# Attention and feed-forward on one core: Q of groups 2 to 5 by pairs of heads, as 2x2 blocks in seven block products, with the sums on GpSimd

## The chip, the cores and the metric

The kernel runs on one core of a Trainium2 chip. The core has five engines with a queue of instructions each: TensorE (PE in the profile; PEld is its load of weights, which overlaps), VectorE (DVE), ScalarE (ACT), GpSimd (POOL) and SyncE (SP), which here only issues DMA transfers. An engine works through its queue in order and waits at an instruction until what it depends on is there. PSUM is the memory that TensorE writes into, in banks of 128 x 512 floats; SBUF is the working memory.

The metric is the time of one launch on the device in microseconds (us); the median of the runs counts.

## What is computed

Two layers on x of shape (2, 512, 512): attention with 32 query heads and 8 key/value heads of 128, causal softmax, an output projection, a residual and a layer norm; then a feed-forward of a base matrix and eight low-rank experts with a sparse routing, a residual and a layer norm. All in float32. Cut to what matters for the change:

```python
q = (x @ Wq).reshape(B, S, 32, 128).transpose(0, 2, 1, 3)     # B=2, S=512, HIDDEN=512
k = jnp.repeat((x @ Wk).reshape(B, S, 8, 128).transpose(0, 2, 1, 3), 4, axis=1)
v = jnp.repeat((x @ Wv).reshape(B, S, 8, 128).transpose(0, 2, 1, 3), 4, axis=1)
scores = jnp.where(causal, jnp.einsum('bhqd,bhkd->bhqk', q, k) * scale, -inf)
out = jnp.einsum('bhqk,bhkd->bhqd', jax.nn.softmax(scores), v)
x = layernorm(x + out.transpose(0, 2, 1, 3).reshape(B, S, 4096) @ Wo)
x = layernorm(x + ffn(x))
```

## The kernel before

Float32 accuracy comes from float16 matmuls: every operand is kept as a high and a low float16 part, and a product is three matmuls (high x high, high x low, low x high) that add up in one PSUM bank (`mm3`, L227). The weights are scaled by a power of two for each tile and then cut into the two parts by GpSimd (`split16`, L115: a scaling at L119, the high part at L121, the low part at L122). A result in PSUM is cut by ScalarE (high part, L234) and VectorE (low part, L235) in `cut_psum`.

The work goes over the 8 key/value heads ("groups" g, with 4 query heads each) and the two batches b: (0,0), (0,1), (1,0), ..., (5,1), then (6,0), (7,0), (6,1), (7,1). Each (g, b) has four units i = 0 to 3, one for each 128 query rows. One step of the main loop (L947) has, in the order in which the program is written:

- `unit_a` (L332) of this unit: the scores of four heads into banks `s`, the row maxima on VectorE (L395), the exponential on ScalarE (L400), and the cut of the weights of the softmax into the tile `phl` (ScalarE L359, VectorE L362), a transpose by DMA into `pt` after each half (`sync_transpose`, L388)
- one projection or two of the next (g, b): K and Q of head 0 in unit 0, Q of head 1 in unit 1, V in unit 2, Q of heads 2 and 3 in unit 3 (L956). Each is 12 matmuls of 512 columns (`project`, L242) into a bank of tag `pj`, of which there are two; the sums of squares `tot` (`total`, L127), from which the scales of the weights come, take banks of the same tag. After V, four copies and a transpose put its parts in order (`turn_v`, L301). `factors` (L256) puts five small GpSimd instructions (`lm`, L261 and L265) ahead of a group's products.
- `unit_b` (L415) of the unit before: softmax times V, `pv`
- `unit_c` (L456) of the unit before that: times Wo, `pw`, added into `acc` by VectorE (L469)

Between these stand the pieces of work that prepare weights for a later group: `prepare` (L159) loads six tiles (K, V, four of Q), `measure` (L176) takes their maxima on VectorE (L125), squares and sums them (`tot` on TensorE, `scales` on VectorE, L133), and `split16` cuts them. `at(generator, steps)` (used at L886 to L898) says in which steps of the main loop a piece is written into the program. The framework's scheduler then decides the order on each engine up to the tail, whose order is written out by hand (L910). The loads stand in SyncE's queue together with the transposes. The feed-forward's weights are loaded and prepared by `ffn_setup` (L474), on GpSimd above all, in the steps 20 to 36; its loads take buffers of the tag `raw`, which the projections' weights use too.

Of the kernel before, what the change touches and what calls it, by code (L numbers as in the profile page):

```python
# [25 lines left out]
NL = NE * NR + NE  # L26
SCALE = float(P) ** -0.5
# [4 lines left out]
TOP = 15  # L32
CUT = 2.0**-18
# [7 lines left out]
def kernel(  # L41
# [68 lines left out]
    def split(hi, lo, view):  # L110

        nc.gpsimd.tensor_scalar(hi, view, 1.0, 1.0, ALU.mult, ALU.mult)
        nc.gpsimd.tensor_tensor(lo, view, f(hi), ALU.subtract)
# [19 lines left out]
    def scales(sc, tot, n):  # L133

        nc.vector.tensor_scalar(
            tot[:, :n].bitcast(I32), tot[:, :n].bitcast(I32), 24, 23,
            ALU.logical_shift_right, ALU.logical_shift_left,
        )
        nc.vector.tensor_scalar(sc[:, 0, :n], tot[:, :n], 2.0**-109, 2.0 ** (64 - TOP), ALU.max, ALU.mult)
        nc.vector.reciprocal(sc[:, 1, :n], sc[:, 0, :n])  # L140
# [18 lines left out]
    def prepare(g, js, raws=None):  # L159

        if raws is None:
            raws = [load_raw(source(g, j), f"{g}_{j}", j >= 6) for j in js]
            yield
        name = f"{g}_{js[0]}"
        rows = js[0] >= 6
        n = 1 if rows else 6
        if (g, rows) not in SC:
            yield from measure(g, js, raws, name, rows, n)
        sc = SC[(g, rows)]
        for k, (j, raw) in enumerate(zip(js, raws)):  # L170
            j = 0 if rows else j
            LAST[(g, js[k])] = split16(*w_tile(g, js[k]), raw, sc[:, 1, j : j + 1], g == 0)
            if k % 2:
                yield

    def measure(g, js, raws, name, rows, n):  # L176
# [12 lines left out]
        scales(sc, total(sq, n, name), n)  # L189
        SC[(g, rows)] = sc  # L190
        yield

# [16 lines left out]
    def convert_x(b):  # L209

        raws = [load_raw(xt[b, :, c, :], f"x{b}_{c}") for c in range(KC)]
        yield
        yield from split_x(b, raws)

# [114 lines left out]

    PT = {}  # L330

    def unit_a(g, b, i, whole=True):  # L332
# [7 lines left out]
        phl = sb.tile([P, nb * P], F16, tag="PHL", name=f"phl{g}_{b}_{i}", bufs=2)  # L340
# [5 lines left out]
        def cut_p(h):  # L346
            nc.vector.reciprocal(st[:, 2, h : h + 2], st[:, 1, h : h + 2])
# [4 lines left out]
            for j in (h, h + 1):  # L352
                src, by = es[j], st[:, 3, j : j + 1]
                n = full + (j + 1) * R
                p = phl[:, (j * m + (j == 3)) * P :]
# [31 lines left out]
            on = slice(0, 2 * m) if h == 0 else slice(2 * m, nb)  # L387
            sync_transpose(pt[:, on], phl[:, on.start * P : on.stop * P])  # L388
# [85 lines left out]
    def ffn_setup():  # L474
# [6 lines left out]
        lars = [sb.tile([P, 512], F32, tag="raw", name=f"lraw{k}", bufs=6)[:, : half * NL] for k in range(2)]  # L481
        for k, lar in enumerate(lars):
            sync_load(lar.rearrange("p (c n) -> p c n", c=half), lar_in[:, k * half : (k + 1) * half, :])
        lraw = load_raw(lora_b, "lorab")
# [28 lines left out]
        scales(fsc, tot, 4)  # L513
# [360 lines left out]
    def first_rows():  # L874
        yield
        for k in (2, 3):
            w_squares(mx[:, 17 + k : 18 + k], wo_raw[k])
        amax(sq1[:, 1:2], mx[:, 17:21])
        tot = total(sq1[:, 1:2], 1, "2")
        sc = sb.tile([P, 2, 8], F32, tag="sc2", name="sc2")  # L880
        scales(sc, tot, 1)
        SC[(0, True)] = sc
        yield
        yield from prepare(0, ROWS, wo_raw)
# [5 lines left out]
    at(late_x(1, (1, 3)), 5, 6, 7, 7)  # L890
    at(ffn_setup(), 20, 21, 21, 21, 22, 22, 28, 28, 29, 29, 36)
    for g in range(1, NG):
        u = NT * (starts[g] - 2) - (3 if g == NG - 2 else 0)
        if g > 1:
            at(prepare(g, JS), u - (1 if g == NG - 2 else 2), u, u, u + 1, u + 2, u + 2, u + 3, u + 3, u + 3)
        u += NT
        if g > 1:
            at(prepare(g, ROWS), u - 2, u, u + 1, u + 2, u + 2, u + 3, u + 3)  # L898
# [48 lines left out]
    for s in range(len(units) - NT):  # L947
        if s < len(units):
# [6 lines left out]
            if nx:  # L955
                for j in ((4, 0), (1,), (5,), (2, 3))[i]:  # L956
                    proj(*nx, j)
# [72 lines left out]
```

## Time and profile before

| What | us |
|---|---|
| median of 3 runs (665.70 to 666.60) | 665.71 |
| the profiled execution, its own time | 665.56 |
| its span on the core (granted TensorE clock 0.999) | 663.7 |
| matmuls of `pw`, all 768 | 177.2 |
| matmuls of `pq`, all 672 | 152.4 |
| matmuls of `pv`, all 960 | 105.6 |
| matmuls of the scores, all 768 | 101.6 |
| GpSimd: low parts of weights (L122), 70 of 512 columns | 79.6 |
| GpSimd: scalings of weights (L119), 70 of 512 columns | 47.7 |
| GpSimd: high parts of weights (L121), 66 of 512 columns | 39.7 |

The durations of matmuls overlap one another (a matmul of 512 columns has 0.379 us, but its successor starts 0.216 us after it), so sums by group show shares, not time on a clock. Where time is meant, it is read from starts. The times of the four units of one group and batch in the middle of the program, busy time of each engine in each stretch:

```
stretch (us)    length  PE     DVE   ACT   POOL
282.90:293.70   10.80   10.80  5.60  4.32  2.44    unit 0
293.70:300.50    6.80    6.80  5.67  4.38  0.00    unit 1
300.50:308.70    8.20    8.20  7.17  6.56  1.42    unit 2
308.70:321.00   12.30   12.30  8.87  6.86  9.50    unit 3
```

A group takes the two batches, so about twice the sum of such a column. DMA issues of 256 KB land after 3.5 to 5.4 us by the page, the transposes after 3.7.

### The profile page before, as it was taken

What the parts mean: (1) busy time and instruction counts of PE and PEld (TensorE: products, weight loads), DVE (VectorE), ACT (ScalarE), POOL (GpSimd) and SP (SyncE); (2) the same over time, 40 slices, a digit from 0 to 9 for tenths busy, and PEclk for the clock granted to TensorE, in tenths of its full rate; (3) what the DMA queues carried; (4) which work ended last, traced back from release to release, by engine and by line L of the source; (5) the groups of instructions that cost most, each with busy time, mean ns of one, the idle gap of its engine ahead of it and who ended that gap; (6) DMA issues with size and microseconds to landing.
All of it is one profiled execution on the core that took longest, in us unless ns stands there. A gap on an engine that the chain in (4) does not pass through costs nothing.

```text
span 663.7 us, 12446 instructions
## 1 busy us (share of the span) xinstructions
PE 649.9 (98%) x3948; PEld 373.8 (56%) x3948; DVE 519.7 (78%) x1695; ACT 387.9 (58%) x1198; POOL 261.3 (39%) x411
## 2 busy tenths in 40 slices
PE   9999999999999999999999999999999999999995
PEld 5766556555555555555655555555555556555552
DVE  6797778868697787868698796868687687878796
ACT  6984755657375864747376474737566474545510
POOL 6885550806037199714127167054405001100011
PEclk9999999999999999999999999999999999999999
DMA  8859292827649393836739282754718263563321
GB/s 317 284 86 206 69 238 41 170 62 154 113 95 242 51 225 54 153 68 131 147 66 259 47 189 55 141 113 92 155 29 143 41 129 59 100 120 76 74 42 48
DMA packets 213538, 81.06 MB, mean 122 GB/s; under 512 B 198112, under 2 KB 198368, under 8 KB 213472
## 3 DMA queue, kind: packets, MB, share of 16 engines
q1 hardware_dynamic: 213472, 80.26, 57.4%
q8 instruction: 31, 0.51, 0.3%
q14 instruction: 35, 0.29, 0.1%
HBM read 29.12 MB, written 2.10 MB: 47 GB/s over the span
## 4 chain that ended last, share of the span: by engine, by line
PE 49%; DVE 9%; ACT 5%; issue 2%; DMA 1%; POOL 0%; POOLq 0%; ACTq 0%; DVEq 0%
PE pq L230 13%; PE pw L230 13%; PE pv L230 7%; PE s L230 7%; PE pk L230 4%; PE pvp L230 2%; ACT s L400 2%; DVE phl L362 2%; ACT phl L359 2%; PE pa L230 1%; DVE s L395 1%; DVE acc L469 1%; DMA pt<-phl 1%; DVE y L586 1%; DVE o L235 1%
## 5 line engine op out<-in xcount | busy, mean ns | idle before, releaser
L400 ACT ACTIVATE s<-s,ast 128x320 f32<-128x320 f32 (+15 forms) x256 | 117.8, 460 | 147.0 <-DVE ast L395 143.6
L230 PE MATMUL pw<-w,o 128*128 128x512 f16 x768 | 177.2, 379 | 0.3 <-DVE acc L469 0.3
L230 PEld LDWEIGHTS <-w 128*128 128x128 f16 x1008 | 98.0, 98 | 111.0 <-issue 0.2
L230 PE MATMUL pq<-xT,w 128*128 128x512 f16 x672 | 152.4, 379 | 0.0
L362 DVE SCALAR_TENSOR_TENSOR phl<-s,ast,phl 128x128 f16<-128x128 f32 (+7 forms) x352 | 125.2, 417 | 34.6 <-ACT phl L359 32.4
L359 ACT ACTIVATE phl<-s,ast 128x96 f16<-128x96 f32 (+11 forms) x304 | 117.6, 479 | 5.8 <-DVE ast L349 3.9
L230 PEld LDWEIGHTS <-o 128*128 128x128 f16 x768 | 74.9, 98 | 77.4 <-DVE o L235 0.7
L395 DVE CUSTOM_DVE_ANT_0 s<-s,mask,lm 128x320 f32<-128x320 f32 (+15 forms) x256 | 113.3, 502 | 0.4 <-PE s L230 0.4
L230 PE MATMUL pv<-pt,vt 128*128 128x256 f16 (+1 forms) x960 | 105.6, 262 | 1.0 <-DMA pt<-phl 1.0
L230 PE MATMUL s<-k,q 128*128 128x480 f16 (+15 forms) x768 | 101.6, 279 | 1.8 <-DVE phl L362 1.0
L230 PEld LDWEIGHTS <-vt 128*128 128x128 f16 x960 | 86.0, 99 | 20.7 <-issue 1.6
L230 PEld LDWEIGHTS <-q 128*128 128x128 f16 x768 | 62.5, 98 | 39.8 <-issue 2.7
L261 POOL TENSOR_SCALAR lm<-sc,xs 128x1 f32<-128x1 f32 x16 | 4.2, 265 | 193.9 <-DVE acc L469 101.7
L122 POOL TENSOR_TENSOR w<-raw,w 128x512 f16<-128x512 f32 x70 | 79.6, 1156 | 0.3
L119 POOL TENSOR_SCALAR raw<-raw,sc 128x512 f32<-128x512 f32 x70 | 47.7, 691 | 55.6 <-issue 40.9
L469 DVE SCALAR_TENSOR_TENSOR acc<-pw,lm,acc 128x512 f32<-128x512 f32 x64 | 47.7, 745 | 20.4 <-PE pw L230 20.2
L235 DVE SCALAR_TENSOR_TENSOR o<-pv,o 128x512 f16<-128x512 f32 x64 | 43.6, 681 | 24.3 <-ACT o L234 24.2
L234 ACT ACTIVATE o<-pv 128x512 f16<-128x512 f32 x64 | 40.1, 627 | 30.4 <-PE pv L230 30.3
L400 ACT ACTIVATION_READ_ACCUMULATOR s<-s,ast 128x1 f32 x256 | 51.6, 202 | 0.0
L125 DVE TENSOR_REDUCE mx<-raw 128x1 f32<-128x512 f32 x68 | 43.6, 675 | 2.0 <-DMA raw<-in_wo_dram 2.0
L235 DVE SCALAR_TENSOR_TENSOR q<-pq,q 128x512 f16<-128x512 f32 x56 | 37.3, 682 | 9.8 <-ACT q L234 9.8
L234 ACT ACTIVATE q<-pq 128x512 f16<-128x512 f32 x56 | 34.6, 618 | 12.8 <-PE pq L230 12.7
(172 smaller groups left out, 660.1 us busy)
## 6 DMA issues: line engine op xcount, KB each, us to landing
raw<-in_wo_dram SPq DMA_DIRECT2D x32, 256.0 KB, 3.5
raw<-in_wq_dram SPq DMA_DIRECT2D x29, 256.0 KB, 4.2
xraw<-in_xt_dram SPq DMA_DIRECT2D x8, 256.0 KB, 5.0
raw<-in_wk_dram SPq DMA_DIRECT2D x8, 256.0 KB, 3.7
raw_x<-in_xt_dram SPq DMA_DIRECT2D x8, 256.0 KB, 4.5
acc<-in_x_dram SPq DMA_DIRECT2D x8, 256.0 KB, 5.4
pt<-phl SPq DMA_TRANSPOSE x128, 3.7
out_dram<-y SPq DMA_DIRECT2D x8, 256.0 KB, 2.0
```

Of the source, the lines that this page charges most:

```text
L119: nc.gpsimd.tensor_scalar(view, view, by, 1.0, ALU.mult, ALU.mult)
L122: return first.ins, nc.gpsimd.tensor_tensor(lo, view, hi, ALU.subtract).ins
L125: nc.vector.tensor_reduce(dst, view, AX.X, ALU.max, apply_absolute_value=True)
L230: nc.tensor.matmul(dst, a, b, start=first and j == 0, stop=last and j == n - 1)
L234: nc.scalar.activation(hi, psrc, AF.Copy, scale=by)
L235: return nc.vector.scalar_tensor_tensor(lo, psrc, by, hi, ALU.mult, ALU.subtract).ins
L359: nc.scalar.activation(dst, src, AF.Copy, scale=by)
L362: nc.vector.scalar_tensor_tensor(dst, src[:, at : at + k], by, p[:, at : at + k], ALU.mult, ALU.subtract)
L395: nc.vector.tensor_tensor_reduce(out=sc[:, :n], in0=sc[:, :n], in1=mask[:, S - n :], scale=lm[:, 0:1], scalar=BIG, op0=ALU.add, op1=ALU.mi ...
L400: nc.scalar.activation(sc[:, :n], sc[:, :n], AF.Exp, bias=st[:, 0, j : j + 1], scale=-1.0, accum_out=st[:, 1, j : j + 1])
L469: nc.vector.scalar_tensor_tensor(a, pw, LM[(g, b)][:, 7:8], a, ALU.mult, ALU.add)
L586: nc.vector.tensor_scalar(dst, src, st[:, 0:1], st[:, 2:3], ALU.subtract, ALU.mult)
```

## The change

For groups 2 to 5 (`by_products`) the Q of two heads is computed as a product of a 2x2 block matrix (two heads by two halves of the 512 inputs) with a 2x2 block matrix of x (two halves of the inputs by two halves of the 512 rows), in seven block products instead of eight (the scheme of Strassen and Winograd). One block product is six matmuls of 256 columns. The sums that the scheme needs:

- of the weights, once for a group and pair: `combine_w` on GpSimd, four additions of 256 columns, and seven blocks cut into parts instead of four
- of x, once for a batch: `combine_x` on GpSimd, in the first units
- of the results, for each pair and batch: partly by adding two products up in one PSUM bank, partly on VectorE from PSUM into the float tile `z` (and `u`), partly by three additions on GpSimd. The low part of Q comes from `z` on GpSimd, the high part from ScalarE.

A pair takes four banks of tag `pj` (`one`, `two` in `first_products`; `three`, `four` in `last_products`) where it took two. Unit 0 has K and the first products of pair 0, unit 1 the last products of pair 0 and the first of pair 1, unit 2 the last of pair 1, unit 3 the projection of V, which was in unit 2.

Besides: the tile `phl` is kept in halves with three buffers instead of whole with two; `ffn_setup` goes from the steps 20 to 36 to the steps 45 to 51, with its own buffers in place of those of tag `raw`; the steps at which weights are prepared are changed; the weights of the projections are scaled to a smaller size (`TOP`, `CUT`); Wo and the feed-forward keep theirs (`ROWTOP`).

```diff
@@ -24,13 +24,16 @@
 HPG = 4
 NE, NR = 8, 16
 NL = NE * NR + NE
+HALF = S // 2
+PAIRS = ((0, 1), (2, 3))
 SCALE = float(P) ** -0.5
 NEG = -1.0e30
 BIG = 3.0e38
 EPS = 1e-5
 
-TOP = 15
-CUT = 2.0**-18
+TOP = 13
+CUT = 2.0**-14
+ROWTOP = 15
 
 XTOP = 11
 
@@ -110,7 +113,7 @@
     def split(hi, lo, view):
 
         nc.gpsimd.tensor_scalar(hi, view, 1.0, 1.0, ALU.mult, ALU.mult)
-        nc.gpsimd.tensor_tensor(lo, view, f(hi), ALU.subtract)
+        nc.gpsimd.tensor_tensor(lo, view, hi, ALU.subtract)
 
     def split16(hi, lo, view, by, fast=False):
 
@@ -130,13 +133,16 @@
         nc.tensor.matmul(tot[:, :n], ones, sq[:, :n], start=True, stop=True)
         return tot
 
-    def scales(sc, tot, n):
+    def by_products(g):
+        return 1 < g < NG - 2
+
+    def scales(sc, tot, n, top=TOP):
 
         nc.vector.tensor_scalar(
             tot[:, :n].bitcast(I32), tot[:, :n].bitcast(I32), 24, 23,
             ALU.logical_shift_right, ALU.logical_shift_left,
         )
-        nc.vector.tensor_scalar(sc[:, 0, :n], tot[:, :n], 2.0**-109, 2.0 ** (64 - TOP), ALU.max, ALU.mult)
+        nc.vector.tensor_scalar(sc[:, 0, :n], tot[:, :n], 2.0**-109, 2.0 ** (64 - top), ALU.max, ALU.mult)
         nc.vector.reciprocal(sc[:, 1, :n], sc[:, 0, :n])
 
     W, SC, LAST = {}, {}, {}
@@ -168,6 +174,10 @@
             yield from measure(g, js, raws, name, rows, n)
         sc = SC[(g, rows)]
         for k, (j, raw) in enumerate(zip(js, raws)):
+            if by_products(g) and not rows and k > 1:
+                if k % 2 == 0:
+                    yield from combine_w(g, k // 2 - 1, *raws[k : k + 2], sc)
+                continue
             j = 0 if rows else j
             LAST[(g, js[k])] = split16(*w_tile(g, js[k]), raw, sc[:, 1, j : j + 1], g == 0)
             if k % 2:
@@ -186,9 +196,58 @@
             amax(mx[:, 0:1], mx[:, 1:5])
         sq = sb.tile([P, 8], F32, tag="sq", name=f"sq{name}", bufs=2)
         nc.scalar.activation(sq[:, :n], mx[:, :n], AF.Square)
-        scales(sc, total(sq, n, name), n)
+        scales(sc, total(sq, n, name), n, ROWTOP if rows else TOP)
         SC[(g, rows)] = sc
         yield
+
+    def add(dst, a, b, op=ALU.add):
+        nc.gpsimd.tensor_tensor(dst, a, b, op)
+
+    W2, X2 = {}, {}
+
+    def combine_w(g, p, a, b, sc):
+
+        tiles = [sb.tile([P, 2, KC, P], F16, tag="w", name=f"w{g}_{p}_{k}", bufs=12) for k in range(4)]
+        for raw, j in zip((a, b), PAIRS[p]):
+            nc.gpsimd.tensor_scalar(raw, raw, sc[:, 1, j : j + 1], 1.0, ALU.mult, ALU.mult)
+        w11, w12, w21, w22 = a[:, :HALF], a[:, HALF:], b[:, :HALF], b[:, HALF:]
+
+        def put(k, first, n, view):
+            on = slice(first * HALF, (first + n) * HALF)
+            split(*(tiles[k][:, q].rearrange("p a c -> p (a c)")[:, on] for q in range(2)), view)
+
+        put(0, 0, 2, a)
+        put(1, 1, 1, w22)
+        yield
+        add(w22, w21, w22)
+        put(1, 0, 1, w22)
+        add(w22, w22, w11, ALU.subtract)
+        add(w12, w12, w22, ALU.subtract)
+        yield
+        add(w21, w11, w21, ALU.subtract)
+        put(2, 0, 2, b)
+        put(3, 0, 1, w12)
+        names = ("w11", "w12", "s1", "w22", "s3", "s2", "s4")
+        W2[(g, p)] = {name: tiles[k // 2][:, :, k % 2 * 2 : k % 2 * 2 + 2, :] for k, name in enumerate(names)}
+        yield
+
+    def combine_x(b, raws):
+
+        t = sb.tile([P, 2, 4, 2, HALF], F16, tag=f"xr{b}", name=f"xc{b}")
+        for c in range(2):
+            low, up = raws[c], raws[c + 2]
+            x11, x12, x21, x22 = low[:, :HALF], low[:, HALF:], up[:, :HALF], up[:, HALF:]
+            add(x11, x12, x11, ALU.subtract)
+            add(x12, x22, x12, ALU.subtract)
+            add(x22, x22, x11, ALU.subtract)
+            add(x21, x21, x22, ALU.subtract)
+            for k, raw in ((0, low), (2, up)):
+                split(*(t[:, q, k : k + 2, c, :] for q in range(2)), raw.rearrange("p (a s) -> p a s", a=2))
+            if c:
+                x2 = xT[b]
+                X2[b] = {name: t[:, :, k] for k, name in enumerate(("t1", "t3", "t4", "t2"))}
+                X2[b] |= {"x11": x2[:, :, :2, :HALF], "x21": x2[:, :, 2:, :HALF], "x22": x2[:, :, 2:, HALF:]}
+            yield
 
     xT, XS, CK = {}, {}, {}
 
@@ -211,6 +270,7 @@
         raws = [load_raw(xt[b, :, c, :], f"x{b}_{c}") for c in range(KC)]
         yield
         yield from split_x(b, raws)
+        yield from combine_x(b, raws)
 
     def split_x(b, raws):
         xT[b] = sb.tile([P, 2, KC, S], F16, tag=f"xT{b}", name=f"xT{b}")
@@ -327,6 +387,54 @@
         else:
             end_q(g, b, j, mul_q(g, b, j))
 
+    Z, U = [], {}
+
+    def product(dst, g, b, p, w, x, first=True, last=True):
+        w2, x2 = W2[(g, p)][w], X2[b][x]
+        pairs = []
+        for c in range(2):
+            wh, wl, xh, xl = w2[:, 0, c, :], w2[:, 1, c, :], x2[:, 0, c, :], x2[:, 1, c, :]
+            pairs += [(wh, xh), (wh, xl), (wl, xh)]
+        mm3(dst, pairs, first, last)
+
+    def first_products(g, b, p):
+
+        if not Z:
+            Z.append(sb.tile([P, 2, 4, HALF], F32, tag="base1", name="z"))
+        if p == 0:
+            QT[(g, b)] = sb.tile([P, 2, HPG * NT, HPG, R], F16, tag="Q", name=f"q{g}_{b}", bufs=2)
+        z = Z[0][:, p]
+        u = U[p] = sb.tile([P, HALF], F32, tag="u", name=f"u{g}_{b}_{p}", bufs=2)
+        one = pj(f"one{g}_{b}_{p}")
+        product(one[:, :HALF], g, b, p, "w11", "x11", last=False)
+        product(one[:, HALF:], g, b, p, "s2", "t2", first=False)
+        nc.scalar.activation(z[:, 0], one[:, :HALF], AF.Copy, scale=CUT)
+        nc.vector.scalar_tensor_tensor(u, one[:, HALF:], CUT, z[:, 0], ALU.mult, ALU.add)
+        two = pj(f"two{g}_{b}_{p}")
+        product(two[:, :HALF], g, b, p, "s1", "t1", last=False)
+        product(two[:, HALF:], g, b, p, "s3", "t3", first=False)
+        nc.scalar.activation(z[:, 1:3].rearrange("p a s -> p (a s)"), two, AF.Copy, scale=CUT)
+        add(z[:, 2], z[:, 2], u)
+        add(z[:, 3], z[:, 2], z[:, 1])
+        add(z[:, 1], z[:, 1], u)
+
+    def last_products(g, b, p):
+
+        z = Z[0][:, p]
+        two = pj(f"three{g}_{b}_{p}")
+        product(two[:, :HALF], g, b, p, "s4", "x22", last=False)
+        product(two[:, HALF:], g, b, p, "w22", "t4", first=False)
+        mid = z[:, 1:3].rearrange("p a s -> p (a s)")
+        nc.vector.scalar_tensor_tensor(mid, two, CUT, mid, ALU.mult, ALU.add)
+        one = pj(f"four{g}_{b}_{p}")
+        product(one[:, :HALF], g, b, p, "w12", "x21")
+        nc.vector.scalar_tensor_tensor(z[:, 0], one[:, :HALF], CUT, z[:, 0], ALU.mult, ALU.add)
+        for k, j in enumerate(PAIRS[p]):
+            src = z[:, 2 * k : 2 * k + 2].rearrange("p a (j q) -> p (a j) q", q=R)
+            hi, lo = (QT[(g, b)][:, q, :, j, :] for q in range(2))
+            nc.scalar.copy(hi, src)
+            add(lo, src, hi, ALU.subtract)
+
     PT = {}
 
     def unit_a(g, b, i, whole=True):
@@ -337,13 +445,14 @@
 
         m = 2 * i + 1
         nb = 4 * m + 2
-        phl = sb.tile([P, nb * P], F16, tag="PHL", name=f"phl{g}_{b}_{i}", bufs=2)
         pt = sb.tile([P, nb, P], F16, tag="PT", name=f"pt{g}_{b}_{i}", bufs=2)
         es = []
         st = sb.tile([P, 4, 4], F32, tag="ast", name=f"ast{g}_{b}_{i}", bufs=3)
         full = i * P
 
         def cut_p(h):
+            on = slice(0, 2 * m) if h == 0 else slice(2 * m, nb)
+            phl = sb.tile([P, (on.stop - on.start) * P], F16, tag="PHL", name=f"phl{g}_{b}_{i}_{h}", bufs=3)
             nc.vector.reciprocal(st[:, 2, h : h + 2], st[:, 1, h : h + 2])
 
             nc.vector.scalar_tensor_tensor(
@@ -352,7 +461,7 @@
             for j in (h, h + 1):
                 src, by = es[j], st[:, 3, j : j + 1]
                 n = full + (j + 1) * R
-                p = phl[:, (j * m + (j == 3)) * P :]
+                p = phl[:, (j * m + (j == 3) - on.start) * P :]
                 lows = p[:, full + P :]
 
                 def high(dst, src):
@@ -384,8 +493,7 @@
                     low(lows[:, :full], 0, full)
                 low(p[:, full + (3 - j) * R : full + P][:, : n - full], full, n - full)
 
-            on = slice(0, 2 * m) if h == 0 else slice(2 * m, nb)
-            sync_transpose(pt[:, on], phl[:, on.start * P : on.stop * P])
+            sync_transpose(pt[:, on], phl)
 
         for j in range(4):
             n = full + (j + 1) * R
@@ -478,10 +586,11 @@
         for c in range(KC):
             sync_load(raw[:, c, :], w_base[:, c, :])
         half = KC // 2
-        lars = [sb.tile([P, 512], F32, tag="raw", name=f"lraw{k}", bufs=6)[:, : half * NL] for k in range(2)]
+        rest = sb.tile([P, KC, S], F32, tag="base0", name="fraw")
+        lars, lraw = [rest[:, k, : half * NL] for k in range(2)], rest[:, 2, :]
         for k, lar in enumerate(lars):
             sync_load(lar.rearrange("p (c n) -> p c n", c=half), lar_in[:, k * half : (k + 1) * half, :])
-        lraw = load_raw(lora_b, "lorab")
+        sync_load(lraw, lora_b)
         bias = sb.tile([P, HID + NE], F32, tag="ffnbias", name="ffnbias")
         sync_load(bias, bias_in.broadcast_to([P, HID + NE]))
         sq = sb.tile([P, KC, 4], F32, tag="fsq", name="fsq")
@@ -887,15 +996,23 @@
     at(split_x(0, x0_raw), 1, 1, 2)
     at(prepare(1, JS, w1_raw), 1, 1, 1, 2, 2, 2, 3, 3)
     at(prepare(1, ROWS), 4, 5, 5, 6, 6, 7, 7)
-    at(late_x(1, (1, 3)), 5, 6, 7, 7)
-    at(ffn_setup(), 20, 21, 21, 21, 22, 22, 28, 28, 29, 29, 36)
+    at(combine_x(0, x0_raw), 4, 4, 4)
+    at(late_x(1, (1, 3)), 5, 6, 6, 7, 7, 7)
+    at(ffn_setup(), 45, 46, 46, 46, 47, 47, 49, 50, 50, 51, 51)
     for g in range(1, NG):
-        u = NT * (starts[g] - 2) - (3 if g == NG - 2 else 0)
-        if g > 1:
-            at(prepare(g, JS), u - (1 if g == NG - 2 else 2), u, u, u + 1, u + 2, u + 2, u + 3, u + 3, u + 3)
+        u = NT * (starts[g] - 2)
+        if g == 2:
+            at(prepare(g, (4, 5, 0, 1, 2, 3)), *(u + n for n in (0, 1, 1, 1, 2, 2, 2, 3, 3, 4, 4, 4)))
+        elif by_products(g):
+            at(prepare(g, (4, 5, 0, 1, 2, 3)), *(u + n for n in (-1, 0, 0, 1, 1, 2, 2, 3, 3, 3, 4, 4)))
+        elif g == NG - 2:
+            at(prepare(g, JS), *(u + n for n in (-1, 0, 0, 1, 2, 2, 3, 3, 3)))
+        elif g > 1:
+            at(prepare(g, JS), *(u + n for n in (0, 1, 1, 1, 2, 2, 3, 3, 3)))
         u += NT
         if g > 1:
-            at(prepare(g, ROWS), u - 2, u, u + 1, u + 2, u + 2, u + 3, u + 3)
+            n = (0, 1, 2, 3, 4, 4, 5) if by_products(g) else (-3, -2, -2, -1, 0, 0, 1) if g == NG - 2 else (-2, 0, 1, 2, 2, 3, 3)
+            at(prepare(g, ROWS), *(u + k for k in n))
 
     def advance(last=False):
         while plan.get(s):
@@ -953,8 +1070,12 @@
                 done(unit_a(g, b, i))
             step_live()
             if nx:
-                for j in ((4, 0), (1,), (5,), (2, 3))[i]:
-                    proj(*nx, j)
+                if by_products(nx[0]):
+                    steps = ((proj, 4), (first_products, 0)), ((last_products, 0), (first_products, 1)), ((last_products, 1),), ((proj, 5),)
+                else:
+                    steps = [[(proj, j) for j in js] for js in ((4, 0), (1,), (5,), (2, 3))]
+                for step, k in steps[i]:
+                    step(*nx, k)
                     advance()
             step_live()
         if s >= LB:
```

More of the change, by code (lines that the diff above doesn't have):

```diff
@@ L512, in ffn_setup @@
         fsc = sb.tile([P, 2, 8], F32, tag="fsc", name="fsc")
-        scales(fsc, tot, 4)
+        scales(fsc, tot, 4, ROWTOP)
         sw, sl, se, sbias = (fsc[:, 1, k : k + 1] for k in range(4))
@@ L880, in first_rows @@
         sc = sb.tile([P, 2, 8], F32, tag="sc2", name="sc2")
-        scales(sc, tot, 1)
+        scales(sc, tot, 1, ROWTOP)
         SC[(0, True)] = sc
```

## The prediction

> **What bounds the kernel now.** I read the page's busy times first, then one whole group in a table of windows, then the chain of waits in the same stretch, and last GpSimd's own timeline.
>
> ```profile
> PE 649.9 (98%) x3948; PEld 373.8 (56%) x3948; DVE 519.7 (78%) x1695; ACT 387.9 (58%) x1198; POOL 261.3 (39%) x411
> ```
>
> ```profile
> core 0: us, PE busy (x) PEld busy (x) DVE busy (x) ACT busy (x) POOL busy (x), PEclk, DMA share, GB/s
> 266.90:342.00 75.10, 75.10 (x461) 42.37 (x460) 58.69 (x187) 44.41 (x141) 26.59 (x40) 1.00 0.60 117
> ```
>
> TensorE is busy in all 75.10 us of a group (one g, both batches), at full clock; between 97 and 500 us the gaps between its matmuls add up to about 3 us. So in this stretch every matmul removed is time gained and every new wait of TensorE is time lost. GpSimd works 26.59 of 75.10 us; nobody waits for it now.
>
> ```profile
> 311.08 5.18 PE pq L230 x24
> 316.26 1.80 PE pv L230 x18
> 318.06 2.59 PE pw L230 x12
> 320.65 0.46 PE s L230 x12
> 321.11 2.59 PE pk L230 x12
> ```
>
> The chain (start us, length us, what) is TensorE alone: 24 matmuls of 512 columns in 5.18 us, 0.216 each; 18 of `pv`, mostly 256 columns, in 1.80.
>
> **TensorE's gain.** A pair of heads costs 24 matmuls of 512 columns now (5.18 us). After: seven block products of six matmuls, 42 of 256 columns. The row that is nearest is `pv`'s matmuls of 256 columns: their starts are 0.109 us apart, so 42 x 0.110 = 4.60 us, 0.58 less. Groups 2 to 5, two batches, two pairs: 16 x 0.58 = **-9.3 us**. The weights' load is hidden as in `pv` (98 ns under 109).
> [...]
>
> **What GpSimd gets.** For each group and pair it now has 4 scalings of 512, 4 hi/lo cuts of 512, 6 of 256 and 8 additions of 256 (both pairs together), and for each batch and pair 3 additions to `z` and 2 lows of Q. Prices come from these rows, of the timeline (start us, length us; of xN the sum) and of the groups (total us, mean ns):
>
> ```profile
> 343.02 0.26 POOL L261 TENSOR_SCALAR lm<-sc,xs 128x1 f32<-128x1 f32 x1 [24.82 <-DVE sc L139]
> 343.38 1.34 POOL L265 TENSOR_SCALAR lm<-sc,lm 32x1 f32<-32x1 f32 x4
> 346.13 1.36 POOL L119 TENSOR_SCALAR raw<-raw,sc 128x512 f32<-128x512 f32 x2 [1.40 <-issue]
> ...
> 350.87 1.37 POOL L119 TENSOR_SCALAR raw<-raw,sc 128x512 f32<-128x512 f32 x2
> ```
>
> ```profile
> L742 POOL TENSOR_TENSOR xr<-xraw,xr 128x512 fp32r<-128x512 f32 x4 | 5.1, 1300 | 0.1
> ...
> L496 POOL TENSOR_TENSOR braw<-braw,ident 128x128 f32<-128x128 f32 x4 | 1.8, 454 | 4.8 <-DMA braw<-in_base_dram 4.8
> ...
> L122 POOL TENSOR_TENSOR lar<-lraw,lar 128x272 f16<-128x272 f32 x2 | 1.4, 702 | 0.1
> ...
> L121 POOL TENSOR_SCALAR lar<-lraw 128x272 f16<-128x272 f32 x2 | 0.8, 417 | 0.1
> ```
>
> Two whole tiles take 346.13 to 350.87 = 4.74 us; a scaling is 0.67 of that, a cut of 512 1.71, a low alone 1.13. Subtractions of 272 columns take 0.702, high copies 0.417, so a cut of 256 is 0.37 + 0.64 = 1.01. No float addition of 256 columns is shown: from below 0.454 (128 columns), from above 1.300 (512); the line between these two gives 0.74 at 256, the 272-column subtraction is nearest, so 0.70, and 0.85 as the dear end, since the rows grow with the columns.
>
> **The wait that this makes.** In the changed program's built order, `one` of pair 1 takes the PSUM bank of `three` of pair 0; that bank is free when VectorE has added `three` to `z`, and that instruction waits for the third addition of pair 0's `z` on GpSimd, which stands in GpSimd's queue behind all weights of both pairs. For batch 0 all of it must fit between the sum of squares `tot` (which gives the scale) and `one`.
> TensorE's side, from the score product that `tot` stands in (call it 0) to `one` of pair 1, by rows of the chain: scores 1.71 + 2.35 + 0.46 + 1.07, `tot` 0.11, `pw` 3 x 2.59, `pv` 1.17 + 1.80 + 0.11 + 2.35 + 0.17, V 2.59, K 2.59, and block products (1.31 for a full bank, 0.66 for `four`) 1.31 + 0.66 + 1.31 + 1.31 + 1.31 + 0.66 = **30.8 us**.
> GpSimd's side: it starts at about 1.6 (score product, `tot`, VectorE's scale), then `lm` 1.75 (5 instructions above, with gaps), K and V tiles 4.74, two lows of the previous Q 2.26, 4 scalings 2.67, 4 cuts of 512 6.84, 6 of 256 6.06, 8 additions 5.6 and 0.6 for their dependence on one another, 3 additions to `z` 2.4: 32.9, so it ends at 34.5. VectorE's addition of 512 (0.68) and two hand-overs (0.2) make 35.4. **Late by 4.7 us** in groups 3, 4 and 5. With the 11 additions at 0.454 the 32.9 shrink to 30.2, late by 2.0; at 0.85 they grow to 34.6, late by 6.4; at the row of 512 columns, 1.300, to 39.5, late by 11.3 (some 705 us in all, which I leave outside the range). In group 2 the same sums give 29.6 against 33.35: late by 3.7. I take the middle: 3 x 4.7 + 3.7 = **+17.8 us**. Nothing gives it back: the next group's `tot` hangs on TensorE's own order. What queues behind the waiting VectorE instruction is the softmax of the same unit, so the stall is one of all engines.
> In batch 1 the weights are there; the 9.4 us of GpSimd rows have 19.6 us to run in, so no wait.
>
> **The second wait, PSUM banks.** `two` of pair 0 takes the bank of K. Now the bank after K's is filled only by Q's 24 matmuls one projection later; afterwards `one` (1.31) and one to five `pv` (0.11 each) lie between.
>
> ```profile
> 320.95 2.75 PE L230 MATMUL pk<-xT,w 128*128 128x512 f16 x12
> ...
> 324.88 0.24 ACT L367 CAST phl<-mask 128x64 f16<-128x64 f32 x1 [1.33 <-DMA pt<-phl]
> ...
> 325.51 0.59 ACT L234 ACTIVATE k<-pk 128x512 f16<-128x512 f32 x1
> ...
> 326.14 0.69 DVE L235 SCALAR_TENSOR_TENSOR k<-pk,k 128x512 f16<-128x512 f32 x1
> ```
>
> K's bank is read out until 2.2 to 4.7 us after its last matmul (here 326.83 against 323.70), on average 3.6 in eight such places. 1.3 of it is ScalarE's cast, which waits for a transpose to free `phl`; with `phl` in halves of three buffers that goes, but V's four copies move into the unit before. From below 1.8, from above 3.6, I take 2.8 (the two groups 6 and 7, without that cast's wait, show 2.1 to 2.5). Less a cover of 1.5: 1.3 us. In batch 0 it lies inside the wait for GpSimd; in batch 1: 4 x 1.3 = **+5.2**.
>
> **What I cost at nothing.** ScalarE's added copies (of 256, 512 and two of 512 for a pair, against two of 512; ScalarE is busy 44.41 of 75.10 us); VectorE's 0.48 + 0.68 + 0.48 for a pair against 1.36; the sums of X early on, which GpSimd does in the first units: their cover is its idle time, and without it some 2 us of start. The network's weights, prepared ten units later: 14 loads (3.3 MB) and some 25 us of GpSimd work stand in the last two groups, where GpSimd has 39% or less to do. The loads now stand in SyncE's queue between two transposes of group 5; three of group 7's wait for a buffer there, and the transposes behind them would be late by 1 to 3 us. Taken as 0, bounds -0.5 and +3.
>
> **Sum.** Profiled run 665.56 (span 663.7 and 1.9 around it), 0.15 under the median: 665.6 - 9.3 + 17.8 + 5.2 = **679.3 us**. Own range from the bounds of the additions and of the bank: 656.4 + 4 x 2.0 + 4 x 0.3 = 666 to 656.4 + 3 x 6.4 + 5.4 + 4 x 2.1 = 689; the middle of it, 670 to 687, I expect.
>
> **Rivals.**
> 1. All cover holds: GpSimd's queue behind `lm` is shorter than 26.5 us (1.6 + 1.75 + 26.5 + 0.9 = 30.8 of cover), the banks are free: 665.6 - 9.3 = **656.4**. For it: GpSimd's share would be only (27 + 30)/75 = 76%, and VectorE and ScalarE lose little. Against: additions at 0.454 leave 28.4 behind `lm`. Chance 0.15.
> 2. GpSimd is on time, as in 1, but the bank of K is waited for in both batches: 8 x 1.3 = 10.4, 656.4 + 10.4 = **666.8**, between 663 and 671 as the lag is 2.3 to 3.3. For it: the lag is in the trace, whatever GpSimd does. Chance 0.19.
> 3. Late transposes on top of the main case: the 14 loads before a transpose of group 5, the loads of groups 3 to 6 waiting for buffers that GpSimd frees later, a `pv` that waits, some 2 to 3 us in four places: 679.3 + 10 = **690**. It decides once a load in SyncE's queue waits longer than the 3.7 us of a transpose. Chance 0.09.
> The forecast itself, slower by TensorE's wait for GpSimd: 0.57.
>
> **How the numbers follow.** The time is the forecast's, 679. The range goes from 662 (all of rival 2) to 687; left out are rival 1, most of rival 3 and little of the main case. A measurement here tells 0.2% (1.3 us) from no change. Faster: rival 1 and a fifth of rival 2, 0.18; same: a fourth of rival 2, 0.05; slower: the rest, 0.77.
>
> **What would show it.** Matmuls of 256 columns 0.109 apart in the block products, else the gain is wrong. In groups 2 to 5 one gap of 3 to 5 us on TensorE before `one` of pair 1 in batch 0, put down to VectorE's `z`, and before that VectorE waiting for GpSimd's addition; none in batch 1. Gaps of about 1.3 us before `two` of pair 0 in batch 1. GpSimd busy without a pause for 30 us after each `tot`. If additions of 256 take under 0.5 us, or GpSimd ends before VectorE gets there, the forecast falls and 656 to 667 is right; if gaps before `pv` with a transpose as releaser add up to 10 us, rival 3 is.

## The result, and the profile after

The changed kernel takes 692.66 us (median of 4 runs, 690.12 to 695.45) against 665.94 before: ratio 1.040, 95% interval 1.036 to 1.044. The forecast was slower, 679.3 us with a range up to 687; the direction was right, the size was not. The profiled execution took 693.2 us (span 691.4), 27.6 more than the one before.

The busy times of the changed kernel:

```profile
PE 653.2 (94%) x4236; PEld 404.3 (58%) x4236; DVE 521.7 (75%) x1711; ACT 400.8 (58%) x1230; POOL 403.0 (58%) x603
```

GpSimd has 142 us more to do, TensorE's share falls from 98% to 94%. What TensorE waits for between 97 and 440 us (engine, tile, releaser: us in all, times, longest); before, this list held one wait, of 0.3 us:

```profile
PE one L290 <- DVE z L428: 9.8, 4, 3.0
PE one L290 <- POOL w L116: 3.3, 3, 1.1
PE two L290 <- DVE k L295: 2.1, 5, 0.8
PE pv L290 <- DMA pt<-phl: 2.0, 3, 1.3
...
```

The forecast's two waits are there: `one` of pair 1, four times, and `two` for K's bank. Two things are not in the forecast's sum: `one` of pair 0 waits for weights, and `pv` for transposes.

Where the 27.6 us are, by the starts of the matmuls (start to start, less what the same matmul takes at full clock):

| Part | us |
|---|---|
| block products in place of Q's matmuls, 16 x (5.18 - 42 x 0.109) | -9.6 |
| pauses before `one` of pair 1, batch 0 (1.5, 3.2, 2.8, 2.8) | +10.4 |
| pauses in `one` of pair 0 for its weights, 3 x 1.4 | +4.2 |
| matmuls at half clock behind three of the pauses (1.6, 1.6, 2.8) | +6.0 |
| `two` for K's bank, five times | +2.9 |
| `pv` (4.7) and `tot` (1.2) between 97 and 440 us | +5.9 |
| pauses of over 0.1 us from 440 to 505 us, 5.7 against 1.5 before | +4.2 |
| the first group, up to 97 us | +3.1 |
| not assigned (pauses below 0.1 us, the tail) | about +0.5 |

The third term of the loss is seen in a table of windows: the pause, and the 3.2 us behind it.

```profile
core 0: us, PE busy (x) PEld busy (x) DVE busy (x) ACT busy (x) POOL busy (x), PEclk, DMA share, GB/s
309.90:312.70 2.80, 0.16 (x3) 0.04 (x1) 2.77 (x14) 1.90 (x10) 1.75 (x3) 1.00 0.00 0
313.90:317.10 3.20, 3.20 (x17) 2.20 (x16) 1.40 (x5) 1.73 (x6) 2.27 (x2) 0.50 0.32 64
```

TensorE has 0.16 us of work in 2.8; then its granted clock (the column after POOL) is 0.50, and matmuls of 256 columns start 0.213 us apart in place of 0.109.

GpSimd's queue in group 4, batch 0 (start, us, line), from `lm` to the additions to `z`:

```profile
279.12 0.27 POOL L321 TENSOR_SCALAR lm<-sc,xs 128x1 f32<-128x1 f32 x1
...
307.73 1.78 POOL L116 TENSOR_TENSOR w<-raw,w 128x512 f16<-128x512 f32 x2
309.47 0.73 POOL L204 TENSOR_TENSOR z<-z,u 128x256 f32<-128x256 f32 x1
310.28 0.72 POOL L204 TENSOR_TENSOR z<-z 128x256 f32<-128x256 f32 x1
311.08 0.72 POOL L204 TENSOR_TENSOR z<-z,u 128x256 f32<-128x256 f32 x1
```

It runs without a pause from 274.58 to 311.80; from `lm` to its end it is 32.7 us long (the forecast said 32.9). And VectorE at the same time:

```profile
300.39 0.42 DVE L412 SCALAR_TENSOR_TENSOR u<-one,z 128x256 f32<-128x256 f32 x1 [1.41 <-ACT z L411]
302.75 0.69 DVE L128 TENSOR_REDUCE mx<-raw 128x1 f32<-128x512 f32 x1 [1.94 <-DMA raw<-in_wo_dram]
306.60 1.31 DVE L128 TENSOR_REDUCE mx<-raw 128x1 f32<-128x512 f32 x2 [3.17 <-DMA raw<-in_wo_dram]
308.21 0.69 DVE L128 TENSOR_REDUCE mx<-raw 128x1 f32<-128x512 f32 x1 [0.30 <-DMA raw<-in_wo_dram]
...
312.00 0.69 DVE L428 SCALAR_TENSOR_TENSOR z<-three,z 128x512 f32<-128x512 f32 x1
```

This was in no step of the forecast: VectorE's maxima of Wo's rows wait 5.4 us for their loads, which the changed plan writes two steps later than before. What queues behind them (`o`, `acc`, the softmax) runs late, and L428 starts at 312.00, with no wait of its own, 0.2 us after GpSimd's last addition. So two causes end at the same moment, and the profile names only VectorE. The experiments had to tell them apart.

### The profile page after: what moved, and what is told of

Read it like the earlier page. It is cut to its first block, busy times and chain, and to the rows that moved or that the text cites. A ratio compares the mean times of both kernels' runs of the same rounds, so it can differ in the third digit from the quotient of the medians.

```text
span 691.4 us, 13264 instructions
## 1 busy us (share of the span) xinstructions
PE 653.2 (94%) x4236; PEld 404.3 (58%) x4236; DVE 521.7 (75%) x1711; ACT 400.8 (58%) x1230; POOL 403.0 (58%) x603
## 5 line engine op out<-in xcount | busy, mean ns | idle before, releaser
L290 PEld LDWEIGHTS <-w 128*128 128x128 f16 x1296 | 128.2, 100 | 100.5 <-issue 14.6
L468 ACT ACTIVATE phl<-s,ast 128x96 f16<-128x96 f32 (+11 forms) x304 | 123.3, 479 | 7.6 <-DVE ast L458 5.3
L290 PE MATMUL pv<-pt,vt 128*128 128x256 f16 (+1 forms) x960 | 109.0, 262 | 5.3 <-DMA pt<-phl 3.7
L290 PE MATMUL s<-k,q 128*128 128x64 f16 (+15 forms) x768 | 102.6, 279 | 2.7 <-DVE phl L471 1.7
L290 PE MATMUL pq<-xT,w 128*128 128x512 f16 x288 | 65.9, 379 | 0.8 <-DVE fsc L145 0.8
L204 POOL TENSOR_TENSOR q<-z,q 128x512 f16<-128x512 f32 x32 | 36.5, 1157 | 46.9 <-ACT q L435 46.9
L125 POOL TENSOR_TENSOR w<-raw,w 128x512 f16<-128x512 f32 x54 | 61.4, 1156 | 0.3
L122 POOL TENSOR_SCALAR raw<-raw,sc 128x512 f32<-128x512 f32 x54 | 36.8, 691 | 38.8 <-DVE sc L146 38.0
L290 PE MATMUL pk<-xT,w 128*128 128x512 f16 x168 | 38.9, 379 | 0.0
L290 PE MATMUL pvp<-xT,w 128*128 128x512 f16 x168 | 38.5, 379 | 0.0
```

Of the source, the lines that this page charges most:

```text
L122: nc.gpsimd.tensor_scalar(view, view, by, 1.0, ALU.mult, ALU.mult)
L125: return first.ins, nc.gpsimd.tensor_tensor(lo, view, hi, ALU.subtract).ins
L204: nc.gpsimd.tensor_tensor(dst, a, b, op)
L290: nc.tensor.matmul(dst, a, b, start=first and j == 0, stop=last and j == n - 1)
L468: nc.scalar.activation(dst, src, AF.Copy, scale=by)
```

## The experiments

Each ran in 4 executions (the last one in 10) beside the kernel before; the ratio is to the kernel before, its interval in brackets.

**The additions to `z` on VectorE** (L204 for `z`, all pairs):

```diff
-        add(z[:, 2], z[:, 2], u)
-        add(z[:, 3], z[:, 2], z[:, 1])
-        add(z[:, 1], z[:, 1], u)
+        nc.vector.tensor_tensor(z[:, 2], z[:, 2], u, ALU.add)
+        nc.vector.tensor_tensor(z[:, 3], z[:, 2], z[:, 1], ALU.add)
+        nc.vector.tensor_tensor(z[:, 1], z[:, 1], u, ALU.add)
```

> The changed kernel with the three additions to z of every pair and batch on VectorE instead of GpSimd. Theory: the pauses before pair 1's first product (10.4 us over four groups) are GpSimd's queue, which this takes out of the way, and the half clock behind them (6.0 us) is the pauses' consequence, so both go; the queue also starts some 2 us earlier, so the wait of pair 0's first product for its weights (1.4 us in three groups) shrinks or goes: 692.7 - 10.4 - 6.0 - 0 to 4.2 = 672 to 676 us. Rival A: the half clock belongs to the matmuls of the block products and not to the pause: slow stretches stay, about 680. Rival B: VectorE with 48 additions more (some 20 us over 16 pairs) becomes the one that is waited for: 684 or more.

Measured: 703.14 us, ratio 1.057 (1.054 to 1.061): 10 us slower than the changed kernel, a miss. VectorE in group 4 of this kernel:

```profile
305.51 0.69 DVE L128 TENSOR_REDUCE mx<-raw 128x1 f32<-128x512 f32 x1 [1.86 <-DMA raw<-in_wo_dram]
306.11 0.41 DVE L417 TENSOR_TENSOR z<-z,u 128x256 f32<-128x256 f32 x1
309.07 0.69 DVE L128 TENSOR_REDUCE mx<-raw 128x1 f32<-128x512 f32 x1 [2.55 <-DMA raw<-in_wo_dram]
309.68 0.41 DVE L418 TENSOR_TENSOR z<-z 128x256 f32<-128x256 f32 x1
```

The additions now stand between the maxima that wait for Wo, and the pause before `one` of pair 1 grows to 3.6 us in three groups. GpSimd was taken out of the way and the pause stayed: this is what turned the search to VectorE's queue. In batch 1 the additions delay `tot` (1.75 us, four times) and `one` of pair 1 (0.7 to 1.0, four times).

**The pause filled with work** (13 matmuls whose result nobody reads, ahead of `one` in `first_products`):

```diff
+        if (b, p) == (0, 1):
+            fill = ps.tile([P, HID], F32, tag="wo", name=f"fill{g}", bufs=1)
+            for _ in range(13):
+                nc.tensor.matmul(fill, xT[0][:, 0, 0, :P], xT[0][:, 0, 0, :], start=True, stop=True)
         one = pj(f"one{g}_{b}_{p}")
```

> The changed kernel with 13 matmuls of 512 columns (2.8 us) in front of pair 1's first product in batch 0 of groups 2 to 5, into a bank that nobody reads. Theory: TensorE is given half clock after it has had nothing to do for about 3 us; filled, the pause costs what it did (3.0, and 1.3 more in group 2, where it was 1.5), but the clock stays full behind it: 692.7 - 6.0 + 1.3 = 688, granted clock 0.997 or more. Rival A, half clock from the kind of matmul: stretches of half clock stay, 694. Rival B, the stretches are chance: they turn up elsewhere, 692.

Measured: 697.02 us, ratio 1.047 (1.045 to 1.049), granted clock 0.990. It missed, since the fill itself had to wait 1.6 to 2.4 us in three groups for its bank: for VectorE's addition to `acc`, which stands behind the maxima too. Half clock came again behind the pauses of 2.4 and 2.2 us, not behind the one of 1.6.

**The feed-forward's setup late, alone, in the kernel before** (with the buffers of its own that the change gives it):

```diff
-    at(ffn_setup(), 20, 21, 21, 21, 22, 22, 28, 28, 29, 29, 36)
+    at(ffn_setup(), 45, 46, 46, 46, 47, 47, 49, 50, 50, 51, 51)
```

> The kernel before with only the feed-forward's setup moved to the steps of the change, and into buffers of its own. If its 14 loads in SyncE's queue and its work on GpSimd make the pauses that the changed kernel has between 440 and 505 us (5.9 us against 1.9 before), it costs about 4: 670. If these come from the block products' own delays, it costs nothing: 665 to 667.

Measured: 669.84 us, ratio 1.0054 (1.0039 to 1.0069): 3.6 us, near the 4 expected if the loads and the work are what costs. TensorE in this kernel (start, us, tile, wait before it):

```profile
465.69 0.38 PE L230 MATMUL pw<-w,o 128*128 128x512 f16 x1
468.82 1.44 PE L230 MATMUL pv<-pt,vt 128*128 128x256 f16 x6 [2.76 <-DMA pt<-phl]
```

`pv` waits 2.8 us for a transpose, and from 468.60 to 474.80 the granted clock is 0.50 again. The forecast took 0. The loads do not show as the cause: the setup's first eight leave SyncE's queue by 445.1, twenty us earlier, and `pv` goes on at 468.82 here and at 469.07 in the kernel before. What differs is the work in front of it. In the kernel before, 22 matmuls of Q run from 462.30 to 467.05 and cover the transpose. Here 10 do; the other 12 run from 475.00 on. The setup's sums of squares (`totf`) take a bank of tag `pj`, and eight squares of the setup on ScalarE (0.43 to 0.63 us each) stand between 460.3 and 467.1, so that Q's bank is read out from 469.0 on and not from 464.7. That these two push Q back is read from the order in the trace; no run takes them away alone.

**The sums of x of batch 0 behind Wo's preparation** (`behind_all(combine_x(0, x0_raw), *LAST[(0, 9)])`; only GpSimd's order differs):

> The changed kernel with the sums of x of batch 0 put behind the preparation of Wo of group 0 in GpSimd's queue, all else in the same order on every engine. If the 3.1 us that the changed kernel has lost after its first group are the wait for Wo's low parts: 692.7 - 3 = 689.5. If they are something else, or if the sums only push the next group's weights back by as much: 692 to 693.

Measured: 690.65 us, ratio 1.037 (1.034 to 1.039); by the medians 2.0 us less than the changed kernel, though the intervals overlap. The place is clear by the start of VectorE's addition of the second `pw` of group 0: 55.7 us before, 58.6 with the change, 56.1 here. So 2.5 of the 3.1 us of the start are the sums of x ahead of Wo's low parts.

**Wo's loads two steps earlier** (in the plan of the rows of groups 2 to 5; GpSimd's order unchanged):

```diff
-            n = (0, 1, 2, 3, 4, 4, 5) if by_products(g) else (-3, -2, -2, -1, 0, 0, 1) if g == NG - 2 else (-2, 0, 1, 2, 2, 3, 3)
+            n = (-2, 1, 2, 3, 4, 4, 5) if by_products(g) else (-3, -2, -2, -1, 0, 0, 1) if g == NG - 2 else (-2, 0, 1, 2, 2, 3, 3)
```

> The changed kernel with the loads of Wo's rows of groups 2 to 5 written two steps earlier, where the kernel before had them; GpSimd's order is unchanged. In the changed kernel VectorE waits 3 to 5 us for these loads (its maxima stand in the queue ahead of the addition of pair 0's third bank to z), while GpSimd's additions to z end at nearly the same moment (311.80 us; VectorE comes free at 312.00). Theory V, VectorE's queue is what TensorE waits for: the pauses and the half clock go, 692.7 - 10 - 6 = 676. Theory G, GpSimd's queue alone is: nothing or little, 690 to 692. Theory T, the two are level, and each hides the other: VectorE waits for GpSimd in place of the load, the pause shrinks by some 0.3 us and the small waits behind VectorE (of pv and of tot, some 3 us in all) go: 687 to 690.

Measured: 690.94 us, ratio 1.038 (1.036 to 1.041). VectorE in group 4 here:

```profile
309.76 0.16 DVE L458 SCALAR_TENSOR_TENSOR ast<-ast,s 128x2 f32<-128x2 f32 x1
312.95 0.69 DVE L428 SCALAR_TENSOR_TENSOR z<-three,z 128x512 f32<-128x512 f32 x1 [3.04 <-POOL z L204]
```

The waits for loads are gone, VectorE is ready at 309.9, and now waits 3.0 us for GpSimd's third addition. The pauses before `one` are as long as they were (9.6 us in four waits). Theory V falls; G and T are both left by this run, and T by the two runs together: each cause alone, taken away, leaves the pause.

**Both at once:**

> Both at once: Wo's loads two steps earlier and the additions to z on VectorE. Theory T: only this takes the pauses away: 692.7 - 10 - 6 - 4 (weights of pair 0 in time) and up to 9 lost again by the additions on VectorE in batch 1 (waits of tot and of pair 1's first product, as the run with the additions alone showed): 673 to 682. Theory V: no better than the loads alone, and worse by those 9 us. Theory G: about 680 too, but then the loads alone gave nothing, and the additions alone should not have lost 10 us.

Measured: 687.11 us, ratio 1.032 (1.030 to 1.034); the time is worse than the 673 to 682 expected, but the pauses before `one` in batch 0 are 0.13 to 0.15 us. Of the loss that is left, some 9 us are in batch 1: `tot` waits 1.8 us four times, `one` of pair 1 0.4 to 1.0 three times. `one` of pair 0 still waits for its weights (3.8 us in all).

**The fill, with Wo's loads early:**

> The kernel with Wo's loads earlier, and 13 matmuls of 512 columns (2.8 us) in front of pair 1's first product in batch 0, into a bank that is now free at that time. If a pause of more than 2 us is what brings half clock, no stretch of half clock is left there, and the time is that of the kernel with the early loads less its half-clock stretches (up to 5 us) plus what the fill exceeds the pause by (2.8 less the pause, four times). If half clock is chance, it stays.

Measured: 689.89 us, ratio 1.035 (1.034 to 1.037), granted clock 0.999. Now the fill starts at once. In group 4:

```profile
309.37 2.97 PE L411 MATMUL fill<-xT 128*128 128x512 f16 x13
312.18 0.82 PE L290 MATMUL one<-xT,w 128*128 128x256 f16 x6
312.83 0.82 PE L290 MATMUL one<-xc,w 128*128 128x256 f16 x6
313.49 1.47 PE L290 MATMUL two<-xc,w 128*128 128x256 f16 x12
```

`two`'s 12 matmuls take 1.47 us; behind the empty pause of the changed kernel they took 2.76. No half clock follows any of the four fills, while two of the four pauses of the same kernel without fill had it (granted clock from 97 to 440 us 1.00 and 0.99). So in these two runs half clock came with TensorE's idle time, not with the kind of matmul.

**The weights prepared one step earlier** (with Wo's loads early; the plan of groups 2 to 5 with every step less one):

> The kernel with Wo's loads earlier, and the weights of groups 2 to 5 prepared one step earlier, so that GpSimd's queue starts some 7 us sooner. GpSimd must wait there for tiles of the group before (V's tile is read until some 12 us after the old start), so some 3 us are gained at least. Theory G or T: the pauses of pair 1 and the 1.4 us of pair 0 go, and the half clock with them: 692.7 - 10 - 6 - 4 - 3 = 670 to 674. Theory V: no better than the early loads alone.

Measured: 704.93 us, ratio 1.059 (1.057 to 1.061), a miss. Its waits of TensorE between 97 and 440 us:

```profile
PE s L290 <- POOL q L204: 27.3, 3, 9.4
PE two L290 <- DVE k L295: 2.2, 5, 0.5
```

The wait for `z` is gone, as it had to be; but the last lows of the previous Q now stand behind the new weights in GpSimd's queue, and the scores wait 9.4 us for them. The queue's order, not its length, decides what is late.

**The additions on VectorE for pair 0 of batch 0 alone** (with Wo's loads early; 12 instructions change their engine, everything else keeps its order):

```diff
-        add(z[:, 2], z[:, 2], u)
+        plus = nc.vector.tensor_tensor if b == p == 0 else nc.gpsimd.tensor_tensor
+        plus(z[:, 2], z[:, 2], u, ALU.add)
...
```

> The kernel with Wo's loads earlier, and the additions to z on VectorE for pair 0 of batch 0 alone, 12 instructions in all; every other instruction in the same order. With Wo's loads early VectorE waited 3.0 us for GpSimd's third addition. Theory T: the four pauses (9.6 us in waits) and their half clock (3.3 to 5) go without the price that the additions had in batch 1 (about 8 us): 690.9 - 9.6 - 4 = 677 (675 to 679), no wait of TensorE for z. Theory V: no change, 691. Rival: GpSimd's queue, relieved of three additions, is still what the next wait hangs on (weights of pair 0, Q's lows): 682 to 686.

Measured: 678.63 us, ratio 1.018 (1.017 to 1.020), as theory T said (675 to 679). Its waits of TensorE between 97 and 440 us:

```profile
PE pv L290 <- DMA pt<-phl: 3.2, 2, 1.8
PE one L290 <- POOL w L116: 2.5, 3, 0.8
PE two L290 <- DVE k L295: 1.5, 4, 0.4
PE tot L133 <- ACT sq L198: 1.3, 3, 0.4
...
PE one L290 <- DVE z L429: 0.2, 1, 0.2
```

12 instructions are worth 12.3 us: 9.6 of pauses down to 0.2, and no stretch of half clock between 97 and 440 us (granted clock 1.00). This settles that, with Wo's loads early, these three additions at the end of GpSimd's queue are what TensorE waits for.

**The same, with the sums of x late and the high parts of K's and V's weights on ScalarE:**

> The same with the sums of x behind Wo's preparation (2.0 us gained in the run with that alone) and the high parts of K's and V's weights on ScalarE in groups 2 to 5, which takes 1.2 us off GpSimd's queue ahead of pair 0's weights (TensorE waits 2.7 to 3.3 us for these in three groups): 677 - 2 - 3 = 672 (670 to 675). If the scheduler's other order costs as much as it gains: 675 to 678.

Measured: 672.55 us, ratio 1.010 (1.008 to 1.013), as expected. The wait of `one` of pair 0 for its weights falls from 2.5 to 0.8 us. It is the best version of the change tried, and still 6.5 us over the kernel before.

**The same, with the setup's loads spread over three steps:**

> The same with the base matrix's loads of the feed-forward's setup spread over three steps instead of one. If it is the block of loads between two transposes that costs the 3.6 us seen in the kernel before with the setup late, 2 to 3 us less than the run without it: 669 to 670. If it is the setup's work itself (its sum of squares on TensorE and the wait for its scale): no change.

Measured: 675.22 us, ratio 1.015 (1.013 to 1.017): no gain, rather 2.7 us lost (the two intervals touch), which neither reading of the expectation has. The sum of squares of the setup now waits for ScalarE (2.2 us), with half clock behind it (granted clock of the whole execution 0.994 against 0.997). Where in the program this setup would cost nothing was not found.

**The kernel before with `phl` in halves, alone:**

> The kernel before with only phl in halves of three buffers. In the changed kernel TensorE waits 3.7 to 5.8 us in all for transposes at pv, which it did not before. If the halves bring that: 668 to 670, with waits of pv for transposes between 97 and 440 us. If it comes from V's projection in unit 3 and the queue that this changes: 665 to 667, or up to 1 us faster, since ScalarE's cast no longer waits for a transpose.

Measured: 665.99 us (10 runs), ratio 1.0004 (0.9994 to 1.0013), and no wait of `pv` between 97 and 440 us. The halves cost nothing in the kernel before; that the waits of `pv` in the changed kernel come from V's projection in unit 3 and from Wo's loads in SyncE's queue is argued, not shown.

## Why the prediction was wrong

Point by point:

- **TensorE's gain, -9.3 us: right.** The matmuls of the block products start 0.109 us apart, and Q's other matmuls 0.216. In the best version the stretch from the second `pw` of (1,0) to that of (4,1), with 14 of the 16 pairs in it, takes TensorE 262.4 us against 264.2 before, by the starts of the matmuls, though its pauses there add up to some 7 us more. That is a gain of some 8.7 where 14 x 0.60 = 8.4 were expected. It is there, and it is eaten.
- **GpSimd's queue, +17.8: right in mechanism, a little too dear.** Queue 32.7 us against 32.9, TensorE's way to `one` 31.1 against 30.8. It shows as 10.4 before `one` of pair 1 and 4.2 in `one` of pair 0, which waits for the same queue at another place: 14.6. The additions of 256 columns that I priced at 0.70:

```profile
L204 POOL TENSOR_TENSOR z<-z,u 128x256 f32<-128x256 f32 x32 | 23.2, 725 | 7.4 <-ACT z L416 6.1
L116 POOL TENSOR_TENSOR w<-raw,w 128x256 f16<-128x256 f32 x24 | 16.1, 672 | 0.0
```

- **"So the stall is one of all engines", and no more: the step that failed most.** I priced a wait of TensorE at its own length. Behind three of the four pauses before `one` of pair 1 (3.2, 2.8 and 2.8 us) the granted clock was 0.50, which cost 1.6, 1.6 and 2.8 us: +6.0 us in the profiled execution. The profile of before could not show it: its longest pause in the middle is 1.2 us and its clock is 1.00 there. The spread of the changed kernel over 690 to 695 us goes the same way: the granted clock of the whole execution is 0.994 in the fastest and 0.987 in the slowest. In the changed kernel's trace the clock reads 0.50 for 3.41 us behind two of these pauses (from 231.93 and 313.85 us on) and for 6.83 at the last one (from 392.36 on, of which the first 1.1 still fall into the pause); the three stretches begin 81.92 and 78.51 us apart, 24 and 23 times 3.41.

The idle time in front of them need not be in one piece. I cut the changed kernel's trace from 60 to 540 us along these multiples of 3.41 us, and counted a matmul of 512 columns as 0.216 us of work, one of 256 as 0.109, and so on. Of 135 pieces at full clock, three were followed by half clock: those in which TensorE was idle for 2.30, 2.31 and 3.18 us in sum; the most among the others was 1.54. In the kernel before, where the clock stays full, no 3.41 us between 60 and 540 hold more than 1.19 of idle time. The length of a single pause does not decide: one of 3.1 us that fell into two pieces, 1.36 and 1.74 us, left the clock at 1.00 in both (first two lines, the kernel with Wo's loads early), and half clock followed a piece in which all pauses together make 1.29 us (last two lines, the kernel with the sums of x late). PE busy in these lines counts every matmul to its modelled end, so its idle time reads shorter:

```profile
core 0: us, PE busy (x) PEld busy (x) DVE busy (x) ACT busy (x) POOL busy (x), PEclk, DMA share, GB/s
229.29:232.71 3.42, 2.06 (x21) 1.76 (x19) 1.34 (x9) 2.71 (x12) 3.34 (x5) 1.00 0.00 0
232.71:236.12 3.41, 1.67 (x16) 1.49 (x16) 2.01 (x8) 1.29 (x3) 1.88 (x3) 1.00 0.00 0
...
452.99:456.40 3.41, 2.12 (x20) 1.21 (x19) 3.24 (x13) 2.39 (x8) 3.41 (x5) 1.00 0.64 119
456.40:459.81 3.41, 3.41 (x10) 1.21 (x9) 2.27 (x15) 2.28 (x13) 3.41 (x5) 0.50 1.18 205
```

- **The bank of K, +5.2: too dear.** Where I looked (group 4, batch 0), K's bank was read out 1.8 us after its last matmul, the lower bound, and not 2.8; in batch 1 the four waits are 0.3 to 0.5 us, all five together 2.9.
- **"What I cost at nothing": wrong in three places.** The sums of x have no cover in the first units (GpSimd is busy 38.4 of the 40 us from 20 to 60: +2.5), the setup late costs 3.6 us alone, though the trace shows no delay by the loads that were named, and `pv` and `tot` wait 5.9 us more in all. For the first two the text named the cover and the price without it, 2 and up to 3 us, and then put neither into the sum.
- **Wo's loads: not seen.** The plan's new steps put Wo's loads behind transposes and just ahead of their maxima. In the trace of before these maxima hardly wait, and I did not follow their loads through the changed queue. It cost little by itself only because GpSimd was as late. VectorE's waits between 97 and 505 us, before and after (us in all, times, longest):

```profile
DVE mx L125 <- DMA raw<-in_wo_dram: 1.4, 2, 1.0
DVE mx L128 <- DMA raw<-in_wo_dram: 16.3, 10, 4.3
```

Sum: 679.3 + 6.0 (clock) + 5.9 (`pv`, `tot`) + 4.2 (440 to 505 us) + 3.1 (start) - 3.2 (GpSimd) - 2.3 (bank) = 693.0; the profiled execution took 693.2. Rival 3, late transposes on top of the main case, was the nearest in time (690), though most of its 10 us were paid elsewhere.

## What to carry to other kernels

Where TensorE is the bound and never pauses, price a new wait at its length plus what a halved clock takes behind it (here 1.6 to 2.8 us behind three pauses of some 3 us), and look at the idle time in sum, not at the longest single pause: in the changed kernel's trace half clock followed the pieces of 3.41 us with 2.30 us of it or more, and none with 1.54 or less. When work is given to an engine that is idle half the time, follow what is already in its queue in order: here, once Wo's loads were early, three short additions at the end of a queue of 33 us cost 12 us, and moving the whole queue earlier only made other work late. When one cause is taken away and the time stays, look for a second that ends at the same moment before the theory is dropped; the wait list names only the one that came last.

## What the runs showed of the hardware

An addition of 256 columns with two operands in SBUF took VectorE 0.43 us where GpSimd stood still, and 1.27 where GpSimd worked on two operands. From the kernel with all additions on VectorE, first VectorE, then GpSimd at the same time (275.73 to 278.00):

```profile
277.02 1.27 DVE L417 TENSOR_TENSOR z<-z,u 128x256 f32<-128x256 f32 x1
278.32 0.43 DVE L418 TENSOR_TENSOR z<-z 128x256 f32<-128x256 f32 x1
```

```profile
275.73 2.27 POOL L204 TENSOR_TENSOR q<-z,q 128x512 f16<-128x512 f32 x2 [8.85 <-ACT q L435]
```

The long addition ended 0.3 us after GpSimd did. The 48 additions of that kernel took 0.73, 0.73 and 0.65 us on average (L417, L418, L419). Two of GpSimd's low parts took 2.61 us there, from 264.26 on, where 2.27 was usual; that VectorE's additions did this is not shown. The kernel before has no such addition between 97 and 500 us. VectorE's additions to `acc`, with one operand in PSUM, took 0.745 us on average there: 0.744 for the 6 during most of which GpSimd worked on two operands, 0.746 for the 37 others.
